# Loads of raw weight slices issued two a slot and stores of prepared weights in four parts, in a mixture-of-experts kernel built on two-level Strassen-Winograd products

## The chip, the cores and the metric

The kernel runs on one core of a Trainium2 chip. The metric is the device time of one execution in microseconds (us), and the time of a kernel is the median of its runs. One execution is also recorded by the hardware profiler; the readings below come from its page and its trace. Engines are named as in the profile: PE is TensorE's matmul, PEld its weight load, DVE VectorE, ACT ScalarE, POOL GpSimd, and SPq the queue of SyncE, which issues nearly all DMAs. A line number such as L186 is a line of the kernel's file.

## The reference: what is computed

The input x has 2 samples of 2048 tokens with 512 features, all in float32. The first layer is a gated mixture: two shared dense blocks, and one expert block that each sample picks by a label. With relu between the two weights of a block:

```python
def _dense(x, wi_, wo_):
    return jax.nn.relu(x @ wi_) @ wo_          # 512 -> 2048 -> 512
s0 = _dense(x, swi[0], swo[0]); s1 = _dense(x, swi[1], swo[1])
h  = jax.nn.relu(jnp.einsum('bsd,bdf->bsf', x, wi[type_label]))
eo = jnp.einsum('bsf,bfd->bsd', h, wo[type_label])
gate_in = jnp.concatenate([eo[:, 0], s0[:, 0], s1[:, 0]], axis=-1)
w = jax.nn.softmax(jax.nn.relu(gate_in @ g1) @ g2, axis=-1)[:, :, None, None]
x = x + eo * w[:, 0] + s0 * w[:, 1] + s1 * w[:, 2]
```

The second layer multiplies by a 512 x 512 matrix and adds a bias, both picked per sample by a category, and adds the input once more: `x = x + x @ W[cat] + b[cat]`.

## The kernel before, in words

**Units.** The tokens are cut into 4 blocks of 1024. A unit is one block through one block of weights: units 0 to 3 use the first shared weights (e = 0), units 4 to 7 the second (e = 1), units 8 and 9 the expert of sample 0 (e = 2), units 10 and 11 that of sample 1 (e = 3). A unit has a first product (`up`, the 512 x 2048 weight `wi`) and a second product (`down`, the 2048 x 512 weight `wo`).

**Products and slots.** Each product is done by a Winograd form of Strassen's scheme on two levels: 7 x 7 = 49 small products (i, k) instead of 64. Each needs one weight tile of 128 x 512 numbers, 256 KB. Some of those tiles are blocks of the weights, the others sums and differences of blocks, prepared beforehand. The emission of the program goes by slots. In `up` each (i, k) takes two slots, 98 in all, with two matmul calls a slot (four records in the profile, since a float32 matmul has two). In `down` each takes one slot, 49 in all, with four calls (eight records). A counter, `clock`, goes up by one in each slot.

**Weight tiles.** A pool of 12 tiles holds them. When TensorE has used one, `used_w` calls `fetch_w`, which issues the DMA for the tile that comes 12 later. All of these are issued from SyncE's queue, in the order in which the program emits them, among all else that this queue issues: the x parts of the first product (`fetch_parts`, 896 KB for each i), stores, and the raw loads below. SyncE executes in order: an instruction that waits, or that can't be issued, holds up all behind it.

**Preparing weights: class Prep.** The sums for e = 1 to 3 are made in the background by GpSimd while TensorE works on earlier units. There is one Prep for each e and each of the two weights (`kind` 0 is `wi`, 1 is `wo`), six in all, worked off in order (`prep_bg`). Each has four slices g. For a slice:
- `begin` takes the buffer `raw` (1 MB, one buffer) and issues the loads of the raw weights into it: 8 DMAs of 128 KB in rows of 512 bytes (L186). It puts 12 steps into the list `p`: four sums `o` (128x384), four sums `s` (128x512), both read from raw, and four sums `t` (128x512), read from `s`. Each step is one sum on GpSimd (L141) and two small writes as a rest (L149).
- Ahead of the first step (`len(p) == 12`), `can` asks for 6 slots since `begin`.
- Five slots after the last of four sums is emitted, `flush` stores the four sums with one DMA (L236): 768 KB for `o`, 1 MB for `s` and for `t`, in rows of 512 bytes, to `ws` in device memory, from where `fetch_w` reads them later. A sums' tile has one buffer; ahead of its next use `view` flushes what is due to be stored from it.
- `more` begins the next slice when the 8 steps that read raw have been emitted and 5 slots have passed since the last of them, or when the list is empty.
- `over` says that a Prep is done: no slices, steps or stores left. Then the next Prep takes its place.

**Pace.** `prep_paced` runs once a slot. It calls `flush`, adds the slot's rate to a pace that is kept to at most 4, and emits a step for each whole unit of pace while `step` succeeds. The rates of the first product stand in `RATE_UP`, one for each i: row 0 for units 4 and later, row 1 for units 0 to 3. In the second product the rate is 0 and `RUN_DN` names the few slots in which `prep_run` emits steps (6 a unit from unit 4 on, 14 before). Steps that fail there are not made up for later, since the debt is set to 0 in the next slot without a count.

**Ends.** Prep(1, 0) begins its first slice in slot 30 of unit 0's second product, and the list `prep_bg` is filled in that product's last slot. If a weight tile is due whose sums are not stored, or when unit 8 ends, `force` emits all that is missing at once (a forced drain).

**Other lines used below.** L809 are the first product's matmuls, L944 the second's, L826, L832, L837, L787 sums of VectorE for the first product, L384 the sums of x on GpSimd (units 0 to 3 alone), L348 the fetch of x parts, L485, L487, L489, L494 and L499 fetches of weight tiles, L1043 the store of a unit's result (2 MB).

Of the kernel before, what the change touches and what calls it, by code (L numbers as in the profile page):

```python
# [15 lines left out]
P = 128  # L16
# [20 lines left out]
def cond_resid_kernel(  # L37
# [22 lines left out]
    nc = tc.nc  # L60
    B, S, D = x.shape
    E, _, F = wi.shape
# [23 lines left out]
    def read_ids():  # L86
# [5 lines left out]
        for b in range(B):  # L92
# [21 lines left out]
    ws = {  # L114
        (e, kind, part): dram.tile(
            [P, 12 if part == "o" else 16, 512], F32, name=f"ws_{e}_{kind}_{part}"
        )
        for e in range(NE)
        for kind in range(2)
        for part in "ost"  # L120
    }
# [9 lines left out]
    def sums_a(eng, pick, put):  # L131


        a11, a12, a21, a22 = pick(0, 0), pick(1, 0), pick(0, 1), pick(1, 1)
        for o, i0, i1, op in (
            (put(5), a21, a22, ADD),
            (put(7), a11, a21, SUB),
            (put(6), put(5), a11, SUB),
            (put(3), a12, put(6), SUB),
        ):  # L140
            eng.tensor_tensor(o, i0, i1, op)  # L141
            yield
# [3 lines left out]
    def rest(count):  # L146

        for _ in range(count):
            nc.gpsimd.memset(idle, 0.0)  # L149

    class Prep:
# [4 lines left out]
        def __init__(self, e, kind):  # L156
# [2 lines left out]
            self.left = {part: NG for part in "ost"}  # L159
            self.p, self.late, self.reading, self.free, self.since = [], [], 0, 0, 0  # L160

        def begin(self):
            if not self.todo:
                return
            g = self.todo.pop(0)
            self.since = clock[0]
            e, kind = self.e, self.kind
            t = bigp.tile([P, 2048], F32, tag="raw", bufs=1, name=f"pr_{e}_{kind}_{g}")

            raw = t.rearrange("p (q b d f) -> p q b d f", q=4, b=2, d=2)  # L170
            cols = slice(g * P, (g + 1) * P)
            for c in range(DC):
                if kind == 0 and e < 2:
                    src = swi_v[:, e * DC + c, :, cols]
                elif kind == 0:
                    src = wi_v[:, bass.ds(label[e - 2] * DC + c, 1), :, cols]
                    src = src.rearrange("p o r f -> p (o r) f")
                elif e < 2:
                    src = swo_v[:, e * 4 + c, g, :].rearrange("p (r f) -> p r f", r=4)
                else:  # L180
                    src = wo_v[:, bass.ds(label[e - 2] * 4 + c, 1), g, :]
                    src = src.rearrange("p o (r f) -> p (o r) f", r=4)
                src = src.rearrange("p (c d) f -> p c d f", c=2)
                a, b = divmod(c, 2)
                for k, q in enumerate((1, 2) if a else (0, 3)):
                    nc.sync.dma_start(out=raw[:, q, b, :, :], in_=src[:, k, :, :])  # L186
            place = lambda n: SLOT_A[n] - 4
            quad = {(0, 0): 0, (1, 0): 1, (1, 1): 2, (0, 1): 3}
            own = {}

            def view(part):
                if part not in own:
                    self.flush(1 << 30, part)
                    own[part] = bigp.tile(
                        [P, 1536 if part == "o" else 2048], F32, tag=part, bufs=1,
                        name=f"p{part}_{e}_{kind}_{g}",
                    )
                form = {
# [3 lines left out]
                }[part]  # L202
                return own[part].rearrange(form, s=4, f=P, **({"b": 2} if part == "s" else {}))

            def line(part, pick, put):
                gen = sums_a(nc.gpsimd, pick, put)

                def op(k):
                    next(gen)
                    rest(2)  # L210
                    if part != "t":
                        self.reading -= 1
                        self.free = clock[0] + 5
                    if k == 3:
                        self.late.append((clock[0] + 5, part, g, own[part]))

                return [lambda k=k: op(k) for k in range(4)]

            self.p += line(
                "o", lambda r, c: raw[:, 0:3, r, c, :], lambda n: view("o")[:, :, place(n), :]  # L220
            )
            self.p += line(
                "s", lambda r, c: raw[:, quad[r, c]], lambda n: view("s")[:, place(n)]
            )
            self.p += line(
                "t", lambda r, c: view("s")[:, :, r, c], lambda n: view("t")[:, :, place(n)]
            )
            self.reading = 8

        def flush(self, now, only="ost"):  # L230
            for job in list(self.late):
                due, part, g, t = job
                if due > now or part not in only:
                    continue
                self.late.remove(job)
                nc.sync.dma_start(  # L236
                    out=ws[self.e, self.kind, part][:, :, g * P : (g + 1) * P],
                    in_=t.rearrange("p (n f) -> p n f", f=P),
                )
                self.left[part] -= 1  # L240

        def step(self):

            self.flush(clock[0])
            done = self.can()
            if done:
                self.p.pop(0)()
            self.more()
            return done

        def can(self):
            return bool(self.p) and (len(self.p) != 12 or clock[0] >= self.since + 6)

        def more(self):
            if self.reading == 0 and (not self.p or clock[0] >= self.free):
                self.begin()

        def over(self):
            return not (self.todo or self.p or self.late)

        def force(self, part):
            self.more()
            while self.left[part]:
                if self.p:
                    self.p.pop(0)()
                self.more()
                if not self.p:
                    self.flush(1 << 30)
# [184 lines left out]
    clock = [0]  # L453
# [194 lines left out]
    prep_bg, other_bg = [], []  # L648
# [9 lines left out]
    def prep_step():  # L658
        done = prep_bg[0].step()
        if prep_bg[0].over():  # L660
            prep_bg.pop(0)
        return done
# [3 lines left out]
    def prep_paced(rate):  # L666
        clock[0] += 1
        if prep_bg:
            prep_bg[0].flush(clock[0])
        pace[0] = min(pace[0] + rate, 4.0) if prep_bg else 0.0  # L670
        while prep_bg and pace[0] >= 1 and prep_step():
            pace[0] -= 1
# [81 lines left out]
    def up(n, xg, tops, y):  # L754
# [12 lines left out]
        for j, i in enumerate(I_UP(n)):  # L767
# [32 lines left out]
            for s, (bk, k, d) in enumerate(SEQ_UP):  # L800
# [77 lines left out]
                if s in top_at:  # L878
                    next(tg, None)
                prep_paced(RATE_UP[n in MAKES][j])  # L880
                if n or j or s >= 7:
                    step(other_bg)
# [10 lines left out]
    def down(n, H, tops, y, prepare):  # L893
# [124 lines left out]
        for s, (i, name) in enumerate(SLOTS_DN):  # L1018
            if s in at:
                for _ in job:  # L1020
                    pass
                job = jobs[at[s]]()
                y_sums(0, *sums.get(at[s], ()))
            elif s in second:
                y_sums(1, *sums.get(second[s], ()))
            slot(i, name)
            next(job, None)
            if name == "z2" and i != 1:
                next(job, None)
            prepare(s)  # L1030
            prep_paced(0.0)
            prep_run(RUN_DN[n in MAKES].get((i, name), 0))
            step(other_bg)
# [188 lines left out]
    def last_layer1(blk, y):  # L1222
# [8 lines left out]


    RATE_UP = [
        [0.36, 0.36, 0.36, 0.36, 0.24, 0.24, 0.36],
        [0.0, 0.24, 0.24, 0.3, 0.3, 0.3, 0.3],
    ]
    RUN_DN = [
# [5 lines left out]
    with tc.manual_schedule():  # L1243
# [18 lines left out]
        for n, (e, blk) in enumerate(units):  # L1262
# [45 lines left out]
            if e >= 2:  # L1308
                b = e - 2
# [41 lines left out]
```

## Time and profile before

| | |
|---|---|
| median of 3 runs (lowest to highest) | 2233.98 us (2233.8 to 2234.62) |
| the profiled execution | 2238.57 us |
| its span | 2236.8 us |
| TensorE's mean granted clock | 0.997 |
| busy: PE, DVE, POOL, ACT | 2190.2, 1622.4, 803.1, 544.7 us |
| bytes moved by DMA, mean rate | 581.59 MB, 260 GB/s |
| issues of tiles from `ws_t`, `ws_s`, `ws_o` | 352, 270, 264, of 256 KB each |
| stores of prepared weights (`ws_s<-ps`, `ws_t<-pt`, `ws_o<-po`) | 24 each; 1024, 1024, 768 KB; 6.4, 8.7, 6.7 us from issue to landing |
| loads of raw slices (`pr<-...`) | 192 of 128 KB; 2.9 to 3.3 us to landing |

How to read it: the table's rows come from the page's parts on busy time and on DMA issues. In a timeline, a line has the start, the time taken, the engine, the source line and the instruction, with "x8" for eight records in a row; "[2.74 <-DMA w<-ws_t]" means that the engine stood idle for 2.74 us just before and that a DMA into a weight tile ended it. For SPq the time is that of the issuing instruction; an issue that can't go ahead is seen as a long one. The list of waits has for each pair the sum, the number and the longest. Matmuls overlap, and the page models their ends, so lost time on PE is read from start to start.

### The profile page before, as it was taken

How to read it: one execution, taken by the hardware profiler on the slowest of the kernel's cores; microseconds unless marked ns; L12 is line 12 of the kernel's file. 1: busy time of each engine (PE TensorE's matmuls, PEld its weight loads, DVE VectorE, ACT ScalarE, POOL GpSimd, SP SyncE). 2: the span in 40 equal slices, each digit the busy share in tenths (PEclk: the TensorE clock that was granted, in tenths of full speed). 3: DMA queues.
4: the chain of work that ended last, by engine and by line, in shares of the span. 5: the costliest groups of instructions: out<-in, count | busy, mean ns of one | idle time of the engine just before them, and what ended most of it. 6: DMA issues, size and time to landing. Idle time of an engine off the chain costs nothing.

```text
span 2236.8 us, 29225 instructions
## 1 busy us (share of the span) xinstructions
PE 2190.2 (98%) x9808; PEld 1850.2 (83%) x9808; DVE 1622.4 (73%) x2043; ACT 544.7 (24%) x937; POOL 803.1 (36%) x1259
## 2 busy tenths in 40 slices
PE   8999999999999999999999999999999999999999
PEld 6787888888888888888888888888777877887785
DVE  7897786687587587578488588587666746767595
ACT  3321231231321321321231230231143133113310
POOL 5887433753741541440450451360032023003300
PEclk9999999999999999999999999999999999999999
DMA  9853997997996996996996997896895696579671
GB/s 342 318 182 107 328 319 223 336 328 237 291 308 204 329 302 199 297 326 184 291 317 208 306 297 234 278 334 206 298 293 178 186 329 217 155 254 322 204 279 54
DMA packets 484065, 581.59 MB, mean 260 GB/s; under 512 B 28361, under 2 KB 316105, under 8 KB 480717
## 3 DMA queue, kind: packets, MB, share of 16 engines
q1 hardware_dynamic: 480188, 572.90, 79.1%
q10 hardware_dynamic: 3728, 6.82, 0.9%
q8 instruction: 80, 1.31, 0.2%
q14 instruction: 69, 0.56, 0.1%
HBM read 421.80 MB, written 157.81 MB: 259 GB/s over the span
## 4 chain that ended last, share of the span: by engine, by line
PE 80%; DVE 8%; DMA 4%; issue 1%; POOL 1%; SPq 1%; ACT 0%; DVEq 0%; POOLq 0%; ACTq 0%
PE dx L944 23%; PE ux L809 20%; PE dy L944 12%; PE uy L809 10%; PE dz L944 6%; PE po L1125 5%; PE uz L809 5%; DMA w<-ws_s 1%; DVE h L915 1%; DMA g1raw<-in_L_cond_g_dram 1%; SPq L186 1%; DVE hid L1065 1%; DVE h L787 1%; DVE t L747 1%; DVE t L749 1%
## 5 line engine op out<-in xcount | busy, mean ns | idle before, releaser
L809 PE MATMUL ux<-xs,w 128*128 128x256 f32 x1792 | 431.5, 382 | 15.8 <-DVE sm L1088 3.2
L809 PEld LDWEIGHTS ux<-xs,w 128*128 128x128 f32 x1792 | 338.4, 191 | 79.6 <-DVE uz L826 6.9
L944 PE MATMUL dx<-t,w 128*128 128x256 f32 x1680 | 397.3, 379 | 3.6 <-DVE ds L966 3.6
L944 PEld LDWEIGHTS dx<-t,w 128*128 128x128 f32 x1680 | 318.2, 190 | 48.6 <-DVE ds L966 2.4
L1162 POOL TENSOR_TENSOR mix<-mix 128x512 f32<-128x512 f32 x72 | 102.1, 1418 | 462.3 <-ACT mix L1157 447.2
L832 DVE TENSOR_TENSOR us<-ux,h 128x512 f32<-128x512 f32 x240 | 162.6, 686 | 125.6 <-PE ux L809 125.2
L915 DVE TENSOR_TENSOR h<-h,h 128x1024 f32<-128x1024 f32 x192 | 246.6, 1299 | 0.0
L781 ACT ACTIVATE h<-h 128x1024 f32<-128x1024 f32 x156 | 164.4, 1055 | 232.8 <-DVE h L837 110.9
L809 PE MATMUL uy<-xs,w 128*128 128x256 f32 x896 | 214.1, 380 | 2.6 <-DVE h L856 2.3
L837 DVE TENSOR_TENSOR h<-uy,us 128x512 f32<-128x512 f32 x168 | 116.1, 691 | 121.9 <-ACT us L830 117.5
L692 POOL TENSOR_TENSOR seen<-pulse 1x1 f32<-1x1 f32 x33 | 16.9, 513 | 511.5 <-DVE pulse L691 471.1
L809 PEld LDWEIGHTS uy<-xs,w 128*128 128x128 f32 x896 | 169.7, 190 | 31.6 <-DVE h L856 4.6
L843 ACT ACTIVATE h<-uz 128x512 f32<-128x512 f32 x168 | 99.5, 592 | 379.7 <-PE uz L809 348.4
L944 PE MATMUL dy<-h,w 128*128 128x256 f32 x672 | 160.0, 381 | 4.5 <-DVE y L968 4.5
L809 PE MATMUL ux<-xi,w 128*128 128x256 f32 x640 | 152.4, 381 | 5.1 <-DVE us L832 2.2
L856 DVE TENSOR_TENSOR h<-uy,us 128x512 f32<-128x512 f32 x168 | 113.0, 687 | 51.3 <-PE uy L809 49.2
L944 PEld LDWEIGHTS dy<-h,w 128*128 128x128 f32 x672 | 127.5, 191 | 23.2 <-issue 5.2
L944 PE MATMUL dz<-h,w 128*128 128x256 f32 x616 | 145.6, 379 | 0.1
L944 PE MATMUL dx<-h,w 128*128 128x256 f32 x616 | 145.5, 379 | 0.0
L809 PEld LDWEIGHTS ux<-xi,w 128*128 128x128 f32 x640 | 120.2, 190 | 25.9 <-issue 7.5
L787 DVE TENSOR_TENSOR h<-h,h 128x1024 f32<-128x1024 f32 x96 | 135.8, 1414 | 6.4 <-ACT h L843 5.1
L141 POOL TENSOR_TENSOR po<-pr 128x384 f32<-128x384 f32 x48 | 54.6, 1137 | 230.9 <-DMA w<-ws_s 56.5
(156 smaller groups left out, 3422.6 us busy)
## 6 DMA issues: line engine op xcount, KB each, us to landing
w<-ws_t SPq DMA_DIRECT2D x352, 256.0 KB, 3.5
w<-ws_s SPq DMA_DIRECT2D x270, 256.0 KB, 4.8
w<-ws_o SPq DMA_DIRECT2D x264, 256.0 KB, 5.1
xs<-xs SPq DMA_DIRECT2D x56, 896.0 KB, 7.0
ws_s<-ps SPq DMA_DIRECT2D x24, 1024.0 KB, 6.4
ws_t<-pt SPq DMA_DIRECT2D x24, 1024.0 KB, 8.7
ys<-y SPq DMA_DIRECT2D x11, 2048.0 KB, 7.9
ws_o<-po SPq DMA_DIRECT2D x24, 768.0 KB, 6.7
```

The costliest lines, as they stand in the source:

```text
L141: eng.tensor_tensor(o, i0, i1, op)
L781: nc.scalar.activation(v, v, AF.Relu)
L787: nc.vector.tensor_tensor(o, blk_of(O[22], cc), blk_of(O[21], cc), ADD)
L809: nc.tensor.matmul(p[:, g, :], lhsT=wt[:, 2 * d + g, :], rhs=x_ops[n, i, k], start=first and g == 0, stop=True, skip_group_check=True,)
L832: nc.vector.tensor_tensor(t, p, half(src, 12 if k == 6 else 22, d), ADD)
L837: nc.vector.tensor_tensor(half(dst, 22, d), bank["y", d], t, ADD)
L843: nc.scalar.activation(half(dst, 11, d), p, AF.Relu if i in final else AF.Copy)
L856: nc.vector.tensor_tensor(half(dst, 12, d), p, sn["b", d], ADD)
L915: nc.vector.tensor_tensor(bl(o), bl(i0), bl(i1), SUB)
L944: nc.tensor.matmul(p, lhsT=wt[:, g, :], rhs=op[g], start=first and g == 0, stop=True, skip_group_check=True,)
L1125: nc.tensor.matmul(po[t], lhsT=mixed[c], rhs=l1[blk][0][:, c, :], start=(c == 0), stop=(c == DC - 1),)
L1162: nc.gpsimd.tensor_tensor(m[:, 3, :, :], m[:, 3, :, :], m[:, j, :, :], ADD)
```

## The change

Nothing is computed differently. `begin` no longer issues the 8 raw loads; it appends them to a list, `loads`. `flush` no longer issues a store; it cuts it into four parts of 192 or 256 KB and appends them to `stores`. A new function, `tick`, takes the place of `flush` in `prep_paced`: once a slot it flushes, issues one part of a store if there is any, and up to two loads. `load` sets `since`, and the first step of a slice now waits for the last load and 5 slots after it. A sums' tile that is needed again, and a forced drain, issue all parts at once. The rates of row 0 go from 0.36 to 0.38 and from 0.24 to 0.26.

```diff
@@ begin
-                    nc.sync.dma_start(out=raw[:, q, b, :, :], in_=src[:, k, :, :])
+                    self.loads.append((raw[:, q, b, :, :], src[:, k, :, :]))
@@ flush
-                nc.sync.dma_start(
-                    out=ws[self.e, self.kind, part][:, :, g * P : (g + 1) * P],
-                    in_=t.rearrange("p (n f) -> p n f", f=P),
-                )
-                self.left[part] -= 1
+                v = t.rearrange("p (n f) -> p n f", f=P)
+                o = ws[self.e, self.kind, part][:, :, g * P : (g + 1) * P]
+                some = v.shape[1] // 4
+                for k in range(4):
+                    cut = slice(k * some, (k + 1) * some)
+                    self.stores.append((o[:, cut], v[:, cut], part, k == 3))
+            if now == 1 << 30:
+                while self.stores:
+                    self.store()
+
+        def store(self):
+            o, v, part, last = self.stores.pop(0)
+            nc.sync.dma_start(out=o, in_=v)
+            self.left[part] -= last
+
+        def load(self):
+            o, v = self.loads.pop(0)
+            nc.sync.dma_start(out=o, in_=v)
+            self.since = clock[0]
+
+        def tick(self):
+
+            self.flush(clock[0])
+            if self.stores:
+                self.store()
+            for _ in range(2):
+                if self.loads:
+                    self.load()
@@ step
-            self.flush(clock[0])
@@ can
-            return bool(self.p) and (len(self.p) != 12 or clock[0] >= self.since + 6)
+            if len(self.p) == 12:
+                return not self.loads and clock[0] >= self.since + 5
+            return bool(self.p)
@@ over
-            return not (self.todo or self.p or self.late)
+            return not (self.todo or self.p or self.late or self.stores)
@@ force
+                while self.loads:
+                    self.load()
@@ prep_paced
-            prep_bg[0].flush(clock[0])
+            prep_bg[0].tick()
@@ RATE_UP
-        [0.36, 0.36, 0.36, 0.36, 0.24, 0.24, 0.36],
+        [0.38, 0.38, 0.38, 0.38, 0.26, 0.26, 0.38],
```

More of the change, by code (lines that the diff above doesn't have):

```diff
@@ L160, in __init__ @@
             self.p, self.late, self.reading, self.free, self.since = [], [], 0, 0, 0
+            self.loads, self.stores = [], []
         def begin(self):
```

## The prediction

> **What bounds the kernel now.** I read the page's shares first, then who TensorE waited for, then the time around each wait on TensorE and on SyncE's queue. Times are us from the span's start.
>
> ```profile
> PE 2190.2 (98%) x9808; PEld 1850.2 (83%) x9808; DVE 1622.4 (73%) x2043; ACT 544.7 (24%) x937; POOL 803.1 (36%) x1259
> ...
> DMA  9853997997996996996996997896895696579671
> ```
>
> TensorE is busy for 2190.2 of 2236.8 us, so every edit together can touch only its 46.6 us of idle time. Eight matmul records follow each other every 1.73 us in the timeline, so a slot of the first product (four records) is 0.86 us and a slot of the second 1.73 us. The DMA row runs at 9 in the first half of most units and at 6 or 7 in the second: the first product is where transfers crowd.
>
> The windows of 20 us put about 20 us of the idle time before 220 and about 17 after 1600, where no slice is prepared. Between lie 204 to 1570, with these waits of TensorE:
>
> ```profile
> PE ux L809 <- DMA w<-ws_t: 2.7, 1, 2.7
> PE ux L809 <- DMA w<-ws_s: 2.3, 2, 1.3
> PE ux L809 <- DMA w<-in_L_cond_swi_dram: 2.0, 2, 1.1
> PE ux L809 <- DVE uz L826: 1.5, 2, 1.0
> ...
> PE ux L809 <- DMA w<-ws_o: 0.3, 1, 0.3
> ```
>
> These are waits for weight tiles. One, of 0.93 us, is at 232.66 in unit 1; the other five stand in the first product of units 4, 5 and 6. The longest, with SyncE's queue in front of it (TensorE above, SyncE below):
>
> ```profile
> 949.98 1.89 PE L809 MATMUL uy<-xs,w 128*128 128x256 f32 x8
> 954.62 3.54 PE L809 MATMUL ux<-xs,w 128*128 128x256 f32 x8 [2.74 <-DMA w<-ws_t]
> 957.99 1.03 PE L809 MATMUL uz<-xs,w 128*128 128x256 f32 x4
> ```
>
> ```profile
> 933.31 0.52 SPq L236 DMA_DIRECT2D ws_o<-po  x1
> ...
> 939.43 0.52 SPq L236 DMA_DIRECT2D ws_s<-ps  x1
> 940.16 10.24 SPq L186 DMA_DIRECT2D pr<-in_L_cond_wo_dram  x8
> 950.51 0.38 SPq L485 DMA_DIRECT2D w<-ws_t  x1
> ```
>
> A store of 1 MB is issued in 0.52 us, and the next issue then stands: 6.43 us of the 10.24 are the first load (the chain of waits has it as "SPq L186 6.43"), the other seven follow at about 0.55. For 11 us no weight tile is issued. The tile of 950.51 is needed at 951.7 and lands at 954.5. The same pair stands ahead of the other waits: load groups of 9.57 us at 1118.20 and of 4.50 at 1150.13, the latter after a store at 1144.29 and an issue blocked for 5.02; at 782.61 a tile's issue stands 8.15 us behind a whole store. So the end is set by TensorE, and where it waits in this stretch, by the weight tiles that SyncE holds behind raw loads and stores.
>
> What these waits cost, from start to start with 1.73 per eight records taken off: 787.65 to 790.51, 1.13; 792.31 to 794.51, 0.47; 949.98 to 954.62, 2.91; 954.62 to 957.99, 1.64 more; 1133.19 to 1136.16, 1.24; 1156.11 to 1158.48 (four records, 0.86), 1.51. The sum is **8.90 us**. The 1.64 is slow matmuls: the granted clock is 0.80 in 952 to 956 and 0.72 in 954 to 960, otherwise 1.00.
>
> On that term the Trainium skill differs ("TensorE: Matmul & The Clock Gate", section "HAM oscillation"): it puts the limit at idle gaps of about 3.4 us, and this one was 2.74. By the page the eight matmuls would not slow down and the sum would be 7.26; the trace decides, 8.90.
>
> **The change, part by part.** *Pace.* I counted slots through the code with both versions of the rules; the count for before puts the last store in slot 28 of unit 8's second product, which fits its 1553.5 in the trace. Twelve steps at 0.36 a slot take 33.3 slots, at 0.38 31.6. The wait before a slice's first step grows from 6 slots after begin to 4 (the loads) plus 5. Of it the four last steps of the slice before cover most, and the pace saved up meanwhile (to at most 4) is caught up at once. Between two Preps the extra 3 slots for the parts of the last store come on top. Both are paid for by 0.02 a slot: the first products of units 4 to 8 hold 0.36 x 70 + 0.24 x 28 = 31.9 steps each before and 33.9 after. In the count, unit by unit, the raw slices and stored megabytes of units 4 to 6 agree within 0.25 MB; units 7 and 8 get 0.75 MB more each. The last part goes out in slot 6 of unit 8's second product, 42 slots ahead of the forced drain. So no forced drain, and the same bytes: nothing here moves the end, and GpSimd's 288 sums and their rests stay (0.99 to 1.27 us each).
>
> *Loads.* The same 192, two a slot. The eight that held the queue now stand in four slots, and the tile fetches due there (one in two slots) go between. Unit 5, from 900: the second slice begins in slot 39 instead of 36, its store's four parts in slots 39 to 42, its loads in 40 to 43, so 2 MB are spread with two or three tiles among them, and the first tile behind the burst is one for about 6 slots later, 5.2 us. The measured lateness there was 2.91. In unit 6 store and loads stood in slots 41 and 42; now the parts stand in 39 to 42 and the loads in 44 to 47. In unit 4 the store at 781.97 is cut. Each late tile (0.47 to 1.51) gains 3.5 us or more by the same spreading. Against this, the DMA engines must move the same bytes and spread work only lowers a peak by what they have to spare: busy 0.92 to 0.97 in these first products, they spare perhaps 0.1 to 0.3 us in 3.5 us. If the transfers, not the order, decide, most of the gain is gone.
>
> *First slice.* Prep(1, 0) begins in slot 30 of unit 0 as before, but its loads wait until the list runs, at the end of unit 0: at about 209 to 214 instead of 164.71 to 168.72. GpSimd's first sum, at 210.53, then waits for a landing at about 217, some 6.5 us, and x sums are queued behind it. They have over 15 us in hand (those of the third product end at 211.8 and are needed near 237). DMA share is 0.20 in 200 to 220. I take 0; without that cover the bound is 6.5 us.
>
> *Stores.* 72 become 288: 216 more issues on SyncE. No row has a store of 192 or 256 KB in 512-byte rows; the nearest are tile fetches of 256 KB, 0.38 a piece and 0.47 from start to start in a run (950.51, 950.98, 951.46), and the 1 MB store, 0.52. I take 0.47: 24 in each first product, 11.3 us of SyncE's time in 86. Its bounds on the end are 0 (SyncE idles or is held by transfers anyway) and the price of the third case below. Below nothing is possible only through the order, counted above.
>
> The Trainium skill speaks against these small parts ("DMA: Bandwidth & Descriptors", "Rules for kernel authors": coalesce many small transfers, at least 1 MiB a DMA). With that page's 2.0 us of fixed cost for each, 216 x 2.0 would be 432 us of transfer time, as an estimate and only if they ran one after another. The raw loads of 128 KB, issued 0.4 us apart and landed after 3.2, show that they overlap.
>
> *Waits.* The first part of a store still waits for GpSimd's sums: "SPq L236 <- POOL idle" is 32.9 us in 26 waits, up to 6.4. Behind it stand tile fetches. The last load was issued about 6 slots ahead of the first store's slot in the worst case (a new Prep, four steps at once), and is 10 ahead now, so the wait falls rather than grows. No buffer is added, so raw and the sums' tiles are held 3 to 4 slots longer; the next user is a step that comes later too.
>
> *Sum.* Of the 8.90 us I let one late tile of 1.5 stay and add 0.9 for tiles that are newly late or sums of VectorE that GpSimd's moved steps meet (the two waits for L826 cost 1.5): 8.90 - 1.5 - 0.9 = **6.5 us**. The profiled execution took 2238.57 (span 2236.8 and 1.8 around it), so it would be 2232.1. The runs' median is 2233.98, 4.6 below; I take the same gain off it: **2227.5**.
>
> **Rivals.**
> 1. *The transfers are the bound, or the timed runs have smaller waits* (0.25). For: DMA share over 0.92; the profiled execution is 4.6 us longer than the median, about half of the 8.90. Then the gain is 8.90 - 4.6 - 2.4 = 1.9 or less: **2232**, within 0.2% (about what a measurement of this kernel can tell from no change; 4.5 us). The change not doing what it says (Tile's waits putting the parts back together) ends here too, at 2234.
> 2. *SyncE's own issue becomes the bound* (0.23). Place: the second half of each first product of units 4 to 8, where SyncE issues without a pause (950 to 963). Twelve added parts at 0.47 put its tiles 5.6 us later, against 3.5 us (four slots) won by spreading: 2.1 in each of five units, 10.5, so **2244.5**; half of it gives 2239. It decides from the point where issues and blocked time together fill the 0.86 us of a slot. Against: SyncE waits for TensorE in most of the second product and in parts of the first.
>
> **Numbers.** Forecast 0.52 (2223 to 2229.5), rival 1 0.25 (2229.5 to 2236), rival 2 0.23 (2238.5 to 2250). Faster by over 0.2% 0.52, within 0.25, slower 0.23. The low end: all 8.90 and the 1.5 of L826 gone, 2223.5. The high end takes in rival 1 and the lower part of rival 2: 2241.
>
> **What would show it.** Right: no wait of TensorE for a weight tile over 1 us in units 4 to 6, the granted clock 1.00 at 940 to 960, no run of raw loads over 5 us on SyncE's queue, stores in parts with tiles between. Rival 1: parts and tiles are interleaved, yet tiles land late by as much. Rival 2: SyncE's queue without a gap and without blocked issues, tiles late in units 7 and 8 too. The prediction is wrong if a wait for GpSimd (L384 or L149) of several us appears at 220 to 300, or a drain at the end of unit 8.

## The result and the profile after

| | before | after |
|---|---|---|
| median of 6 runs each (lowest to highest) | 2235.88 us (2233.8 to 2239.14) | 2245.48 us (2244.88 to 2249.9) |
| the profiled execution, its span | 2238.57, 2236.8 us | 2245.42, 2243.6 us |

The ratio is 1.0044, 95% interval 1.0034 to 1.0055: the change makes the kernel slower by 0.44%, 9.6 us between the medians and 6.8 between the two profiled spans. The forecast was 2227.5; the time lies above the range's end of 2241. It stands close to rival 2's 2244.5, but the runs below show that rival 2's mechanism isn't the cause.

Most lines of the code have moved by 28: the first product's matmuls L809 are L837 now, the sums of x L384 are L412, the stores L236 are L250, the raw loads L186 are L255. Of the page after: busy time, the DMA row, and the stores with their number, size and median us to landing.

```profile
PE 2195.6 (98%) x9808; PEld 1854.7 (83%) x9808; DVE 1619.5 (72%) x2041; ACT 544.6 (24%) x937; POOL 813.4 (36%) x1257
...
DMA  9853997996996996996996897896896696579671
...
ws_s<-ps SPq DMA_DIRECT2D x96, 256.0 KB, 5.2
ws_t<-pt SPq DMA_DIRECT2D x96, 256.0 KB, 5.7
...
ws_o<-po SPq DMA_DIRECT2D x96, 192.0 KB, 5.1
```

TensorE does the same work, 5.4 us longer, and the digits of the DMA row are those of before but for five, each one off by one: the shares say nothing of what happened. A part of a store lands 1.2 to 3 us sooner than a whole one did. The waits of TensorE in the stretch from 204 to 1570 (sum, number, longest) say more:

```profile
PE ux L837 <- DMA w<-ws_s: 5.7, 3, 3.7
PE uy L837 <- POOL xi L412: 3.5, 1, 3.5
...
PE uy L837 <- DMA w<-ws_o: 0.6, 1, 0.6
```

Before, there was no wait for GpSimd's sums of x here, and the longest for a weight tile was 2.7. Now there is one wait of 3.5 us for a sum of x (L412) and one of 3.7 for a weight tile.

**Where the time went.** The two programs issue the same matmuls, so the start of the same matmul in both gives a running difference, after minus before. Its steps are (the ends are times of after):

| stretch | difference at its end | step |
|---|---|---|
| unit 0, to 106 | -0.50 | -0.50 |
| unit 1, to 302 | +0.98 | +1.48 |
| unit 2, to 469 | +6.20 | **+5.22** |
| unit 3, to 630 | +6.58 | +0.38 |
| unit 4, to 811 | +6.08 | -0.50 |
| unit 5, to 995 | +1.64 | -4.44 |
| unit 6, to 1137 | +0.32 | -1.32 |
| unit 6, to 1159 | +7.74 | **+7.42** |
| end of unit 6, to 1166 | +6.22 | -1.52 |
| unit 7, to 1321 | +8.02 | +1.80 |
| to 1658 | +7.35 | -0.67 |
| to the end | +6.85 | -0.50 |

The four negative rows of units 4 to 6 are the predicted gain: 0.50 + 4.44 + 1.32 + 1.52 = 7.78. The matmuls around the longest wait of before are in step again, 1.73 apart, and the granted clock is 1.00 in 940 to 960:

```profile
952.61 1.89 PE L837 MATMUL uy<-xs,w 128*128 128x256 f32 x8
954.33 1.89 PE L837 MATMUL ux<-xs,w 128*128 128x256 f32 x8
```

Two new waits cost 5.22 + 7.42 = 12.64 and outweigh it.

**The wait in unit 6.** SyncE's queue of after, with the end of the raw loads and the next store (the issues between are weight tiles):

```profile
1129.47 1.02 SPq L255 DMA_DIRECT2D pr<-in_L_cond_wi_dram  x2
...
1133.90 0.34 SPq L522 DMA_DIRECT2D w<-in_L_cond_swi_dram  x1
1143.65 0.90 SPq L250 DMA_DIRECT2D ws_o<-po  x2
1144.65 0.46 SPq L517 DMA_DIRECT2D w<-ws_o  x1
```

From 1134.24 to 1143.65 SyncE does nothing. Its next instruction is a part of the store of the sums `o`, and GpSimd hasn't made them. GpSimd of after (its rests left out):

```profile
1136.04 1.67 POOL L141 TENSOR_TENSOR po<-pr 128x384 f32<-128x384 f32 x1 [26.28 <-DMA w<-ws_o]
...
1137.97 2.07 POOL L141 TENSOR_TENSOR po<-pr 128x384 f32<-128x384 f32 x1
...
1140.30 2.08 POOL L141 TENSOR_TENSOR po<-po,pr 128x384 f32<-128x384 f32 x1
...
1142.63 0.99 POOL L141 TENSOR_TENSOR po<-pr,po 128x384 f32<-128x384 f32 x1
```

The first sum starts 5.5 us after the last raw load was issued, the fourth ends at 1143.62, and the store follows at once. The weight tiles behind it in the queue come too late. TensorE of after (the wait in brackets):

```profile
1153.42 3.75 PE L837 MATMUL ux<-xs,w 128*128 128x256 f32 x8 [3.74 <-DMA w<-ws_s]
1156.97 2.79 PE L837 MATMUL uy<-xs,w 128*128 128x256 f32 x8
```

Eight records took 3.75 and 2.79 instead of 1.89; the granted clock was 0.62 in 1150 to 1158. SyncE and GpSimd of before, at the same slice:

```profile
1118.20 9.57 SPq L186 DMA_DIRECT2D pr<-in_L_cond_wi_dram  x8
...
1130.97 1.24 SPq L494 DMA_DIRECT2D w<-in_L_cond_swi_dram  x1
1136.30 0.53 SPq L236 DMA_DIRECT2D ws_o<-po  x1
```

```profile
1130.81 1.00 POOL L141 TENSOR_TENSOR po<-pr 128x384 f32<-128x384 f32 x1 [23.51 <-DMA w<-ws_s]
...
1134.59 1.68 POOL L141 TENSOR_TENSOR po<-pr,po 128x384 f32<-128x384 f32 x1
```

The same three times, before and after: from the end of the last load's issue to the place of the store on SyncE 4.44 and 3.75 us, from that issue to the first sum 3.04 and 5.55, the four sums 5.46 and 7.58. So SyncE stood 4.09 before and stands 9.41 now, and the 5.32 more are 0.69 + 2.51 + 2.12.

Over the whole stretch, SyncE's waits for GpSimd's sums (line of the rest L149 that ends each sum), before and then after:

```profile
SPq L236 <- POOL idle L149: 32.9, 26, 6.4
```

```profile
SPq L250 <- POOL idle L149: 42.2, 19, 9.4
```

A long stand isn't enough for a late tile: the second longest of after, 8.8 us from 1339.4, near the end of unit 7's first product, made none late.

**The wait in unit 2.** Here the steps of the first slice of Prep(1, 1) and the last four sums of x meet on GpSimd. GpSimd of after, then TensorE:

```profile
457.38 1.00 POOL L141 TENSOR_TENSOR po<-pr 128x384 f32<-128x384 f32 x1 [16.21 <-DMA pr<-in_L_cond_swo_dram]
...
462.23 0.99 POOL L141 TENSOR_TENSOR po<-pr,po 128x384 f32<-128x384 f32 x1
463.48 1.40 POOL L412 TENSOR_TENSOR xi<-x 128x256 f32<-128x256 f32 x1
```

```profile
464.94 2.91 PE L837 MATMUL uy<-xi,w 128*128 128x256 f32 x8 [3.50 <-POOL xi L412]
467.65 2.70 PE L837 MATMUL ux<-xi,w 128*128 128x256 f32 x8
```

GpSimd stands idle for 16.21 us, until the raw slice lands, with the sums of x behind its first step. GpSimd of before:

```profile
451.90 1.00 POOL L141 TENSOR_TENSOR po<-pr 128x384 f32<-128x384 f32 x1 [11.72 <-DMA w<-ws_t]
...
458.47 1.41 POOL L384 TENSOR_TENSOR xi<-x 128x256 f32<-128x256 f32 x1
```

Before, the loads were issued in one run from 440.76 to 449.15, and TensorE didn't wait. Now the loads are issued from 446.96 to 453.55. In the count of slots the first step stands in slot 75 of the unit's first product instead of 69, the four sums of x in 77 to 80.

The length of this wait is not fixed by the program. The change, e4, e12 and e13 below emit the same work up to the end of unit 2, and their profiled executions wait 3.5, 1.1, 3.5 and 4.7 us here.

### The profile page after: what moved, and what is told of

Its sections match the earlier page's. It is cut to its first block, busy times and chain, and to the rows that moved or that the text cites. A ratio compares the mean times of both kernels' runs of the same rounds, so it can differ in the third digit from the quotient of the medians.

```text
span 2243.6 us, 29474 instructions
## 1 busy us (share of the span) xinstructions
PE 2195.6 (98%) x9808; PEld 1854.7 (83%) x9808; DVE 1619.5 (72%) x2041; ACT 544.6 (24%) x937; POOL 813.4 (36%) x1257
## 4 chain that ended last, share of the span: by engine, by line
PE 80%; DVE 8%; DMA 5%; issue 1%; SPq 1%; POOL 0%; ACT 0%; DVEq 0%; POOLq 0%; ACTq 0%
PE dx L972 23%; PE ux L837 20%; PE dy L972 11%; PE uy L837 10%; PE dz L972 6%; PE po L1153 5%; PE uz L837 5%; DVE h L943 1%; DMA g1raw<-in_L_cond_g_dram 1%; DMA w<-ws_s 1%; DMA ys<-y 1%; DVE hid L1093 1%; DVE t L777 1%; DVE t L772 1%; DMA w<-in_L_cond_W_dram 1%
## 5 line engine op out<-in xcount | busy, mean ns | idle before, releaser
L837 PE MATMUL ux<-xs,w 128*128 128x256 f32 x1792 | 431.2, 382 | 14.2 <-DMA w<-ws_s 4.5
L837 PEld LDWEIGHTS ux<-xs,w 128*128 128x128 f32 x1792 | 338.8, 191 | 76.5 <-issue 12.4
L809 ACT ACTIVATE h<-h 128x1024 f32<-128x1024 f32 x156 | 164.4, 1055 | 231.9 <-DVE h L865 111.0
L837 PE MATMUL uy<-xs,w 128*128 128x256 f32 x896 | 215.4, 381 | 3.7 <-DVE h L884 2.8
L837 PEld LDWEIGHTS uy<-xs,w 128*128 128x128 f32 x896 | 170.2, 191 | 34.5 <-DVE h L884 6.3
L837 PE MATMUL ux<-xi,w 128*128 128x256 f32 x640 | 154.2, 384 | 5.4 <-DVE us L860 1.6
L141 POOL TENSOR_TENSOR po<-pr 128x384 f32<-128x384 f32 x48 | 61.0, 1272 | 256.3 <-DMA pr<-in_L_cond_wo_dram 65.5
L837 PEld LDWEIGHTS ux<-xi,w 128*128 128x128 f32 x640 | 122.0, 192 | 25.7 <-issue 8.4
```

The costliest lines, as they stand in the source:

```text
L809: nc.scalar.activation(v, v, AF.Relu)
L837: nc.tensor.matmul(p[:, g, :], lhsT=wt[:, 2 * d + g, :], rhs=x_ops[n, i, k], start=first and g == 0, stop=True, skip_group_check=True,)
```

## The experiments

Each ratio is to the kernel before on the same chip, timed in five rounds, with its 95% interval. The expectations speak of three theories. A: the two waits for GpSimd cause the loss, since spread loads bring the raw slices later. B: the 216 added issues do (rival 2). C: the new rates do, by moving the steps to other slots.

### The change taken apart

**e1_loads**: the change, with whole stores.

```diff
-                some = v.shape[1] // 4
-                for k in range(4):
-                    cut = slice(k * some, (k + 1) * some)
-                    self.stores.append((o[:, cut], v[:, cut], part, k == 3))
+                self.stores.append((o, v, part, True))
```

> The change with its stores whole again: loads two a slot and the new rates stay, each store is one DMA. Theory A: the loads do the harm. The last of the eight is issued some 5 us later, GpSimd reaches the slice's first sum before it has landed and stands there, and what is queued behind it (sums of x) or waits for its sums (SyncE at the store) comes late for TensorE. Then this is as slow as the change or slower: 2243 to 2250 us, with the wait of 3.5 us for the sums of x in unit 2 still there. Theory B: the 216 more issues on SyncE do it: then 2230 to 2237, near the kernel before (2235.9). Theory C: the rates do it: 2243 to 2247 too, but then e3 is slow as well.

Measured: 2250.37, ratio 1.0054 (1.0038 to 1.0070). SyncE waits for the sums for 41.8 us in 27 waits; TensorE waits for `ws_s` tiles 8.2 us in four. Without a single added issue of a store the kernel is no faster than the change, so B doesn't explain the loss. The wait for sums of x is 1.4 us and not the 3.5 expected; the first step of Prep(1, 1) stands in slot 72 here.

**e2_stores**: the change, with the loads at once.

```diff
-                    self.loads.append((raw[:, q, b, :, :], src[:, k, :, :]))
+                    nc.sync.dma_start(out=raw[:, q, b, :, :], in_=src[:, k, :, :])
@@ can
-                return not self.loads and clock[0] >= self.since + 5
+                return clock[0] >= self.since + 6
```

> The change with its loads at once again, in begin and with the wait of 6 slots as in the kernel before: only the stores in four parts and the new rates stay. Theory A: no slower than the kernel before, 2229 to 2237 us; waits of SyncE for GpSimd stay at some 33 us in all, none over 7. Theory B: slow as the change, 2242 to 2250, with weight tiles late behind runs of parts. Theory C: slow, and e3 too.

Measured: 2232.69, ratio 0.9980 (0.9970 to 0.9990): faster than before, with all of the 216 added issues. SyncE of e2 in unit 6:

```profile
1110.62 4.88 SPq L188 DMA_DIRECT2D pr<-in_L_cond_wi_dram  x8
...
1117.99 1.03 SPq L517 DMA_DIRECT2D w<-ws_o  x2
1125.70 0.90 SPq L250 DMA_DIRECT2D ws_o<-po  x2
```

The eight loads take 4.88 us behind a store in parts, against 9.57 behind a whole one before. SyncE still stands in front of the store, 1119.0 to 1125.70, but 18 us earlier than in the change, and no tile is late for it: TensorE's matmuls from 1141 to 1163 follow each other without a wait. B is out.

**e3_rates**: before, with the new rates alone.

```diff
-        [0.36, 0.36, 0.36, 0.36, 0.24, 0.24, 0.36],
+        [0.38, 0.38, 0.38, 0.38, 0.26, 0.26, 0.38],
```

> The kernel before with the new rates alone (0.38 and 0.26). Theories A and B: within 3 us of the kernel before, 2233 to 2239 us. Theory C (5% more prepared per slot crowds the transfers of the first product): 2242 or more.

Measured: 2243.36, ratio 1.0026 (1.0015 to 1.0036). A had not expected this: with nothing spread and nothing cut, the pace alone costs 0.26%, and TensorE's late tiles grow (`ws_s` 4.8 us in four, `ws_o` 1.5). C holds for whole stores; why these slots are worse than those of before was not found.

**e4_oldrates**: the change with the rates of before (the same diff, reversed).

> The change with the old rates (0.36 and 0.24). By the count of slots the last slice then isn't quite done at the end of unit 8 and its last parts are drained there. Theory A: within 3 us of the change, 2242 to 2249 us, the wait for the sums of x in unit 2 unchanged, since the rates of units 0 to 3 are the same in both. Theory C: back to 2234 to 2238.

Measured: 2244.69, ratio 1.0038 (1.0024 to 1.0051). The number agrees with A, the cause doesn't. The wait for sums of x in unit 2, expected unchanged, is 1.1 us. The profiled execution is up to 4.3 us behind before in units 1 to 5, has no long wait in unit 6, and is 0.8 to 3.3 us ahead from there to the end of unit 8. Then the stores that aren't done are drained at the end of unit 8. SyncE, and VectorE behind it:

```profile
1592.47 5.84 SPq L250 DMA_DIRECT2D ws_t<-pt  x4
1598.35 1.02 SPq L1081 DMA_DIRECT2D g1raw<-in_L_cond_g_dram  x1
```

```profile
1606.07 0.49 DVE L1091 TENSOR_SCALAR hid<-g1raw,gin 128x512 f32<-128x512 f32 x1 [10.66 <-DMA g1raw<-in_L_cond_g_dram]
```

The load of the gate's weights stands behind the drain; VectorE waits for it with the next unit's sums behind, and TensorE waits 9.5 us for those. So the new rates do what the prediction's count said: without them the steps don't get done. The drain costs 8.65 us (from 1.26 ahead of before to 7.39 behind).

From the four: rates alone +0.26%; parts on top of them bring it to -0.20%, spread loads on top to +0.54%, both to +0.44%. Spreading costs (1.0044/0.9980) 0.64% where stores are in parts and (1.0054/1.0026) 0.28% where they are whole, at the change's wait of 5 slots.

### How much spreading, and where

**e6_fouraslot**: `range(4)` in place of `range(2)` in `tick`, so four loads a slot.

> The change with loads four a slot instead of two, so the last is issued 2 slots after begin, not 4; the rest as in the change. Theory A: between the loads at once (2232.7 us) and the change (2245.5): 2235 to 2242. Rival D: the same, so this tells only whether the harm grows with the spread. If it is as slow as the change, the spread is not the measure of it.

Measured: 2237.62, ratio 1.0006 (0.9996 to 1.0016). At once, four, two a slot: 0.9980, 1.0006, 1.0044.

**e7_stores37**: e2 with rates 0.37 and 0.25.

> Stores in four parts, loads at once, and rates of 0.37 and 0.25 (the least at which the count has no drain at the end of unit 8). The kernel before with the new rates lost 0.26%, so half of that step of the rates should be worth up to 3 us here: 2227 to 2233 us. If parts have made the rates harmless: 2232 to 2235, as with 0.38.

Measured: 2233.57, ratio 0.9989 (0.9980 to 0.9998). With parts the rates matter little.

**e8_late_spread**: the loads of e = 1 at once (wait 6), those of e = 2 and 3 spread.

```diff
+            while e < 2 and self.loads:
+                self.load()
@@ can
-                return not self.loads and clock[0] >= self.since + 5
+                return not self.loads and clock[0] >= self.since + (6 if self.e < 2 else 5)
```

> The change, but the raw slices for e = 1, prepared in units 0 to 3, are loaded at once in begin with a wait of 6 slots; those for e = 2 and 3, from unit 3 on, two a slot as in the change. Theory A: the wait of TensorE for the sums of x in unit 2 (3.5 us and 1.4 of slow clock) goes, the waits in units 6 and 7 stay: 2238 to 2243 us. If all the harm is in units 0 to 3, 2231 to 2235; if none is, 2244 to 2249.

Measured: 2244.84, ratio 1.0033 (1.0020 to 1.0046). A miss in part: the wait for sums of x stayed, 2.8 us. With these loads at once the first step of Prep(1, 1) still stands in slot 72, since that Prep begins later: `over` now waits for the last store's parts. The wait in unit 6 stayed too (`ws_s` 6.3 us in two, longest 4.2).

**e12_early_spread**: the opposite, `e > 1` in both places: e = 1 spread, e = 2 and 3 at once.

> The mirror of the run in which only late slices were spread: the raw slices for e = 1 (units 0 to 3) two a slot as in the change, those for e = 2 and 3 at once with a wait of 6 slots; stores in parts and rates as in the change. The harm of spread loads lay mostly in units 6 and 7, so this should lose little against loads at once everywhere (2232.7): 2232 to 2238 us. Over 2241 would mean that each half alone does most of the harm.

Measured: 2236.42, ratio 1.0004 (0.9995 to 1.0013). The wait for sums of x is there as in the change, 3.5 us; late tiles are 1.9 in all. The late tiles, both of them, are in unit 1. So the late tiles of the later units come with spreading the later loads. The wait in unit 2 does not need the first loads spread: it is there in e8 too, and in e15 below.

### The waits taken away

**e13_rates39**: the change with rates 0.39 and 0.27, the control for the next two.

> The change with rates of 0.39 and 0.27, nothing else: the control for the two runs with longer waits. If the longer waits healed the change, this stays at 2241 to 2249 us, with SyncE's waits for GpSimd near 42 us. If moving the steps' slots healed it, 2232 to 2238.

Measured: 2240.01, ratio 1.0020 (1.0011 to 1.0029). A pace faster by 0.01 a slot removes about half of the loss. The wait for sums of x stays (4.7 us); `ws_s` tiles are late by 1.5 only, and SyncE's longest wait for sums is 7.8.

**e5_wait9**: as e13, and a slice's first step 9 slots after its last load in place of 5 (`since + 9`).

> The change with one size altered: the first step of a slice waits 9 slots after the last load, not 5 (rates 0.39 and 0.27, so that by the count the last part still goes out in unit 8, in slot 43 of its second product, as in the kernel before). Theory A: the harm is that steps are emitted ahead of the landing of late loads, so GpSimd stands in front of them and SyncE in front of GpSimd. Four slots more, 3.5 us, take most of that away: SyncE's waits for GpSimd fall from 42 us to under 25, no wait over 5, and the time to 2231 to 2238 us. Rival D (spread loads hurt by the order of transfers itself): no better than the change, 2243 to 2250. Theory C (rates): worse than the change.

Measured: 2234.67, ratio 0.9993 (0.9984 to 1.0002): the loss is gone. No wait for sums of x, since the first step in unit 2 now stands in slot 79, behind three of the four; late tiles 1.6 in all, both in unit 1. But SyncE's waits for sums, expected under 25 us with none over 5, are 29.2 with one of 7.0 and one of 6.4 from 1136.1, and no tile is late for them.

**e9_due9**: as e13, and a store 9 slots after its sums in place of 5.

```diff
-                        self.late.append((clock[0] + 5, part, g, own[part]))
+                        self.late.append((clock[0] + 9, part, g, own[part]))
```

> The change with the store of four sums due 9 slots after the last of them is emitted, not 5 (rates 0.39 and 0.27 as in the run with the longer first wait; by the count the last part goes out in slot 9 of unit 8's second product). GpSimd's steps stand in its queue as in the change; only SyncE comes to the store later. If the carrier is SyncE standing at a store in front of GpSimd's sums, with weight tiles behind it: SyncE's waits for GpSimd fall from 42 us to under 20, the waits of 5 to 7 us in unit 6 go, the wait for sums of x in unit 2 may stay: 2231 to 2239 us. If the carrier is GpSimd's own lateness, or the order of the transfers: 2242 to 2249.

Measured: 2235.14, ratio 0.9999 (0.9989 to 1.0008). SyncE's waits for sums fall to 26.2 us (under 20 was expected; the longest is 7.0), late tiles to 0.9, and the step in unit 2 moves to slot 79 here too, because Prep(1, 0) ends later.

**e14_due7**: the change (rates 0.38), stores 7 slots after their sums.

> The change at its own rates with stores due 7 slots after their sums instead of 5. If SyncE standing at stores is the carrier, two slots (1.7 us a store) take part of the harm: 2236 to 2242 us, SyncE's waits for GpSimd between 30 and 40 us. If not: 2243 to 2249.

Measured: 2239.99, ratio 1.0020 (1.0008 to 1.0031). SyncE's waits fall to 29.3 us in 13; late tiles are 1.6, both in unit 1. What stays is unit 2, with the step in slot 77, amid the sums of x: TensorE waits 3.0 us for one of them at 470 (6.8 in four waits over units 1 to 3).

**e17_wait9_e1**: the change, with only the first slice of Prep(1, 1) waiting 9 slots.

```diff
-                return not self.loads and clock[0] >= self.since + 5
+                return not self.loads and clock[0] >= self.since + (9 if (self.e, self.kind, len(self.todo)) == (1, 1, 3) else 5)
```

> The change, but the first slice of Prep(1, 1) alone waits 9 slots after its last load instead of 5: its four sums are emitted in slot 79 of unit 2's first product instead of 75, behind three of the four sums of x made there. If the slot sets it: no wait for the sums of x (3.5 us idle and 1.4 of slow clock in the change), and 2238 to 2242 us against 2245.5. The later units' steps move by one or two slots, so their waits may differ by 2 us. If the wait stays, it was not the order on GpSimd.

Measured: 2237.45, ratio 1.0007 (0.9997 to 1.0018). One number in one slice of 24 takes away 0.37 of the 0.44%. GpSimd of e17:

```profile
442.26 0.73 POOL L412 TENSOR_TENSOR xi<-x 128x256 f32<-128x256 f32 x1
456.89 1.00 POOL L141 TENSOR_TENSOR po<-pr 128x384 f32<-128x384 f32 x1 [13.89 <-DMA pr<-in_L_cond_swo_dram]
...
462.63 0.73 POOL L412 TENSOR_TENSOR xi<-x,xi 128x256 f32<-128x256 f32 x1
```

The step still waits for its slice until 456.89, but three sums of x are done ahead of it, by 443, and the fourth isn't needed before it is made. TensorE doesn't wait here. In the later units all steps come a slot or two later, and the wait in unit 6 is gone as well: the loads there end at 1124.80, and SyncE stands 4.9 us instead of 9.4 (sum 31.2, longest 5.1). So e17 doesn't price the two waits apart: the slot of one slice in unit 2 sets those of unit 6 too.

### Parts with loads at once

**e10_stores_wait9**: e2 with `since + 9` in place of 6.

> Loads at once, stores in four parts, first step 9 slots after begin instead of 6, the change's rates: what the runs so far point to. Theory A: no wait for sums of x, fewer waits of SyncE for GpSimd than with 6 slots (33.8 us), 2228 to 2233 us against 2232.7 with 6 slots. If the longer wait adds nothing once the loads are early: 2232 to 2235.

Measured: 2232.49, ratio 0.9981 (0.9972 to 0.9990): as e2.

**e11_before_wait9**: before, with `since + 9` in place of 6.

> The kernel before with the first step 9 slots after begin instead of 6, nothing else. If the longer wait alone is worth something, 2229 to 2234 us; if it only repairs what late loads do, 2234 to 2238, as the kernel before. If lost slots matter, over 2238.

Measured: 2240.45, ratio 1.0018 (1.0009 to 1.0027). The last of the three cases expected: a longer wait alone, with whole stores, makes tiles late (3.9, 1.4, 1.0 and 0.7 us). Like e3, it moves slots and loses; the cause is open.

**e15_stores_due9**: e2 with stores 9 slots after their sums.

> Loads at once, stores in four parts and due 9 slots after their sums, the change's rates. If SyncE's standing at stores still costs something with early loads (33.8 us of it at 5 slots): 2227 to 2231 us. If it is covered there: 2231 to 2235, as at 5 slots (2232.7).

Measured: 2241.10, ratio 1.0027 (1.0017 to 1.0038). A miss in the time that separates the two waits: SyncE's waits for sums fall to 12.3 us and no weight tile is late at all, yet the step in unit 2 now stands in slot 76, TensorE waits 4.7 us for a sum of x, and at 470 the kernel is 7.1 us behind before. So the wait of unit 2 is there with no load spread; the slot makes it.

**e16_parts_both_waits**: e2 with wait 9, stores 9 slots after their sums, rates 0.39 and 0.27.

> Loads at once, stores in four parts, first step 9 slots after begin, stores due 9 slots after their sums, rates 0.39 and 0.27 (no drain by the count). Both waits gone: 2226 to 2231 us, SyncE's waits for GpSimd under 20 us, no wait of TensorE for sums of x. If only one of them counts: 2231 to 2235.

Measured: 2235.01, ratio 0.9990 (0.9980 to 0.9999). A miss: SyncE's waits for sums are 12.4 us, longest 3.0, TensorE waits 0.5 at most for a sum of x, and the gain is no more than e2's. Its profiled execution, 2241.09, was the slowest of its runs. With both waits gone something else costs, and it wasn't found.

The best versions are e2 and e10, 0.20% and 0.19% faster than before: stores in parts, loads at once.

The slot of the first step of Prep(1, 1) in unit 2 and TensorE's wait for sums of x, in all profiles: 69: 0 (before, e3); 72: 0 (e11), 0.2 (e7), 1.3 (e2), 1.4 (e1), 2.8 (e8); 73: 0 (e6); 75: 0.6 (e10), 1.1 (e4), 3.5 (after, e12), 4.7 (e13); 76: 4.7 (e15); 77: 3.0 (e14); 79: 0 (e5, e9, e16, e17). In slots 69 and 79 there is no wait, between them it ranges from 0 to 4.7: the order on GpSimd decides whether there can be one, and when the raw slice lands, how long the sums take and where TensorE stands decide its length.

## Why the prediction was wrong, point by point

**Late tiles of units 4 to 6: right.** 6.5 was forecast from 8.90; these units gave 7.78: 4.44 of 4.55 in unit 5, all of 2.75 in unit 6, but only 0.50 of 1.60 in unit 4. The term that was mis-sized stands beside it: 0.9 for tiles newly late and for work that moved steps meet. The two new waits alone cost 12.64.

**Pace: the count was right, its price wrong.** No drain follows, and e4 shows the drain that there would be without the new rates. But "nothing here moves the end" fails: the rates alone cost 0.26% in whole stores (e3), and 0.01 more a slot takes 0.24% off the change (e13 against after). The same bytes in other slots are not the same time.

**First slice: wrong in place, and I took 0.** I had the loads "at about 209 to 214" and GpSimd's first sum at 217. SyncE had a list of earlier issues in hand: the first load went out at 220.79, and the first sum came at 234.34, 24 us later than before instead of 6.5. Unit 1 lost 1.48; how much of it comes from this slice was not tried.

**Waits: the step that failed.** "The last load was issued about 6 slots ahead of the first store's slot in the worst case [...], and is 10 ahead now, so the wait falls rather than grows." It grew, from 32.9 to 42.2 in sum and from 6.4 to 9.4 at the longest. Two things are wrong in this step. The count: the 6 slots reach to the slice's first sum, and the store comes 5 slots behind the fourth, so the worst case before was 11. The distance fell from 11 to 10. And the price: I took a slot for 0.86 us, which is TensorE's pace. SyncE runs at that pace only when it is ahead. In unit 6 it was behind and ran through its backlog: from the last load (1130.49) to the place of the store (1134.24) the 10 slots took 3.75 us instead of 8.6, as the 11 of before had taken 4.44. In that time the slice had to land (5.5 us) and GpSimd to make four sums (7.6). So of the 5.32 us that SyncE stands longer, 0.69 are the shorter distance, 2.51 the later first sum, 2.12 the slower sums. Why the slice landed later behind its last load was not tried.

Of those 7.6, 2.8 came on top: three sums took 1.67, 2.07 and 2.08 where the fourth, and most others, take 1.00. VectorE of after, in that time:

```profile
1135.64 1.22 DVE L815 TENSOR_TENSOR h<-h,h 128x1024 f32<-128x1024 f32 x1
...
1137.97 1.22 DVE L815 TENSOR_TENSOR h<-h,h 128x1024 f32<-128x1024 f32 x1
...
1140.30 1.22 DVE L815 TENSOR_TENSOR h<-h,h 128x1024 f32<-128x1024 f32 x1
```

Each slow sum lies beside one of them, two starting at the same time, and none lies beside the fourth. In unit 2 one of the four sums took 2.09 too. The Trainium skill has this rule ("SBUF — State Buffer", section "Who interferes with whom"): a VectorE instruction with two inputs in SBUF contends with a GpSimd instruction that reads SBUF, and the second to start waits for the whole of the first. These rows agree: 1.07 and 1.08 more, beside 1.22. No run took the VectorE sums away, so this part was read, not tried.

**Sums of x: looked for in one place only.** I asked for them for Prep(1, 0)'s first slice and found 15 us in hand. I didn't ask the same of Prep(1, 1), whose first step moved from slot 69 to 75 by the three added terms that I had named myself (the loads' 4 slots, the 5 behind them, and the parts of the last store). The wait cost 5.22 in unit 2. The sign of a wrong prediction that I named, a wait for GpSimd of several us (L384 or L149), was the right one, at the wrong place: 464 and SyncE's queue at 1143 instead of 220 to 300.

**Stores: right that 0 was the price to take.** Of bounds from 0 to 10.5, e2 shows that the 216 issues don't cost: the kernel with them is faster. Parts do more than I gave them: they let the raw loads behind them through, in the pair above 4.88 us in place of 9.57. Over all groups of eight loads right behind a store of 1 MB or its last part it is 7.0 to 10.3 us before (eleven groups, median 9.0) and 4.0 to 8.3 in e2 (sixteen, median 6.0). So the many small parts won here, and the measurement decides. The raw loads that the prediction has 0.4 us apart are 0.5 to 0.6 apart (an issue takes 0.4), which changes nothing in it.

**Rivals.** Transfers were not the bound: the late tiles went. SyncE's issue was not either (e1, e2). The case that came, SyncE standing at a store whose sums aren't made, was in the text, with the wrong sign. The other, GpSimd's steps ahead of the sums of x in unit 2, was not.

**What is shown and what stays open.** Shown: in the profiled execution the two waits are more than the whole loss; spreading the loads costs 0.64% beside parts at a wait of 5 slots, the dose counts (e6), and the changes that took the two waits away (e5, e9, e17) took away most or all of the loss, though each of them moved other slots too. In e5 and e9 the rates' share of that is e13's 0.24%. With the wait of 9 slots spread loads are within 0.12% of loads at once (e5 and e10). Open: why e3 and e11 lose with whole stores, what is left in e16, and how far the place and the length of the late tile are an accident of the slots that the steps fall in: stands of 7.8, 6.4 and 7.0 us at this slice in e13, e5 and e14 made no tile late, one of 6.6 in e8 did. That it isn't all accident is argued from e1 and e8: these other schedules with spread loads have a long late tile too (3.83 us at 788 in e1, 4.2 in e8).

## What to carry to other kernels

On a queue that executes in order, a distance between a load and the store of what is made from it has to be counted to the store itself and in time on that queue, not in slots of another engine's pace: a queue that is behind runs through the slots and then stands at the store, with all later fetches behind it. When a background step moves, ask in every unit, and not only at the first, which urgent work of the same engine stands behind it. Cutting a store into parts and spreading the loads ahead of the work are two changes, to be tried apart: here the parts, with the new rates, brought 0.20%, and the spreading, at the wait that the change gave it, cost more than that.

## What the runs showed of the hardware

- Before, the issue next behind a whole store of 1 MB in 512-byte rows took 1.8 to 8.2 us (48 stores, median 4.6), where the median of all SyncE's issues from 204 to 1570 is 0.38. After, the issue next behind a part of 256 KB took 0.6 (median; 2.8 at most). Parts landed in 5.2 to 5.7 us (median), whole stores of 1 MB in 6.4 to 8.7.
- TensorE's eight records after an idle time of 2.74, 3.50 and 3.74 us took 3.54, 2.91 and 3.75 us instead of 1.89, and in the latter two cases the next eight 2.70 and 2.79. The granted clock was 0.72 in 464 to 470 and 0.62 in 1150 to 1158. The length of the idle time alone doesn't decide below 3 us. In the stretch from 204 to 1570 of all profiles, none between 1.0 and 1.9 us had such a tail and all nine from 3.0 us on had one. Between 2.0 and 2.8 three had one (2.04 in e1: 3.44; 2.12 in e8: 2.88; 2.74 before) and four had none (2.19 in e3, 2.24 and 2.76 in e8, 2.26 in e11: 1.97 to 1.99). With the tail, the waits cost 1.5 to 1.7 times their length: 5.22 in unit 2 for 3.50, 7.42 in unit 6 for 3.74 and a shorter one of 0.61.
